# Row sums of layer 3's second four heads: matmul strips instead of accumulating DMAs, in a re-ordered four-layer graph network

## The chip, the core and the metric

The kernel runs on one NeuronCore of one Trainium2 chip. The core has engines with instruction queues of their own: TensorE (matmuls; PE in the profile, its weight loads PEld), VectorE (DVE), ScalarE (ACT), GpSimd (POOL) and SyncE (SP, which here only issues DMAs). GpSimd issues DMAs too: indirect gathers and scatters, and DMAs that add to what lies at the destination. The metric is the time of one launch in microseconds on the device.

## The reference, cut to what matters

The input is `x`, 32 samples of 512 nodes with 256 features, and an adjacency matrix of 512 x 512 that all samples share. Four layers follow one another, each as `x = x + layer(relu(layernorm(x)))`: layer 0 is masked attention with four heads of 64, layer 1 an MLP with two graph attention steps, layer 2 graph attention with four heads of 64, and layer 3 graph attention with eight heads of 32. Layer 3 is the one that changes:

```python
e = leaky_relu(e_src[..., :, None] + e_dst[..., None, :], 0.2)
e = e + (beta * log(adj + 1e-6))[:, None, :, :]
e = where(adj > 0, e, neg_inf)
attn = softmax(e, axis=-1)
h = einsum('bhij,bhjf->bhif', attn, x_proj)
x = x + (h in node order) @ W_out.T
```

The softmax has a numerator (weights times values) and a denominator, the row sum of the weights over all 512 keys. How the row sums are formed is what the change touches.

## The kernel before, in words

All work of one sample is written down as steps (`Step`), one per instruction or per small group of matmuls (`q.unit`), by `layer0` to `layer3` for each of the 32 samples. Nothing is issued then. `Plan.order` afterwards simulates the engines with the costs of `cost` and `transfer` and picks, again and again, the step that can start earliest, ties by its due time. `Plan.issue` writes the instructions in that order to all engines. So each engine's instruction order is fixed when the kernel is built, steps of up to seven samples lie between one another, and the semaphores hold an engine wherever the order was too hopeful. Due times come from `PERIOD` (the distance of samples), the longest chain behind the step, and `URGENT`, a table of corrections by tile name and layer; `STARTS`, `PACE` and `LAYERS` say from when a sample and a layer may run. A step starts only where buffers are free: 60 blocks of 128 x 512 fp32 in SBUF (tag `block`: p, total, R, raw and so on share them) and the eight PSUM banks (tag `bank`). A tile holds its buffer until its last reader is done.

For DMAs the planner keeps `landed`, the landing times of the last eight transfers of SP, and starts no SP transfer before the eighth-last has landed (`LANES = 8`). GpSimd's transfers are not held back in this way.

`separable` is the attention of layers 2 and 3. Heads go in groups of four: layer 2 has one group (g = 0), layer 3 two (g = 0 and 1). For each group, four row vectors are spread to all partitions by DMA (`R`), and for each of four key blocks j of 128 keys, and each of the group's four heads s, ScalarE forms `p[s]` (an exponential, 128 keys x 512 queries) and VectorE applies the maximum and the mask. TensorE then multiplies each `p[s]` with that head's values, as four strips of 32 columns side by side into one bank `av` (layer 2: two banks of strips of 64), accumulated over j. The row sums come in three ways:

- `direct`: four more strips behind those of the values, with a matrix of ones as weights, in each key block, into a bank `sm` accumulated over j. Before the change this is used for the last sample in layer 2 and the last two samples in layer 3 (`q.left`).
- `total`, group 0 otherwise: VectorE adds the four key blocks into four blocks; one set of four strips with ones then sums over partitions.
- group 1 of layer 3 otherwise: the key blocks j = 1 to 3 are added into the block of j = 0 (`first[s]`) by a DMA that GpSimd issues (`accum_op=ALU.add`), 12 per sample; one set of strips with ones follows.

`bars` hands the banks on: in layer 3 `normalise` copies them, sends the sums through DRAM for reciprocals, and multiplies. Layer 1 has the gathers that matter for the queues: rows are sorted by an indirect scatter (`order`), partial sums are written to a table in DRAM (`table`), and two gathers per 128 nodes (`g`, and `u`, which adds to what ScalarE wrote) fetch them; all of those are GpSimd's.

Of the kernel before, what the change touches and what calls it, by code (L numbers as in the profile page):

```python
# [18 lines left out]
ALU = mybir.AluOpType  # L19
# [15 lines left out]
H2, F2 = 4, 64  # L35
# [11 lines left out]
NO_TIES = float(N * (N * N - 1) // 3 - N) / 8.0  # L47


PERIOD = 190.0  # L50
STARTS, PACE = (0.0, 0.0, 111.0, 97.0), 58.0
LAYERS = (0.0, 42.0, 210.0, 99.0)

URGENT = {
    "stats:0": -40, "mv:0": -105, "ve:0": 445, "ms:0": -472, "h:0": 223, "pt:0": -138, "hT:0": -14, "qT:0": -396,
    "kT:0": 47, "v0:0": -81, "x:0": -388, "sc:0": 167, "p0:0": 112, "total:0": 519, "av:0": 239, "sm:0": 244,
    "sums:0": -217, "raw:0": 302, "s1:0": -35, "few:0": 258, "s2:0": 28, "oT:0": -33, "stats:1": -176, "mv:1": 83,
    "ve:1": 388, "rs:1": -39, "ms:1": -22, "h:1": -80, "pt:1": 220, "hT:1": 117, "mm:1": -251, "o1:1": -437,
    "nd1:1": -275, "w1:1": -438, "at:1": -24, "base:1": 129, "pick:1": -46, "sq1:1": -121, "ew:1": -778,
    "order:1": -382, "ds1:1": -77, "v1s:1": 27, "ab:1": 187, "past:1": 22, "sm:1": -279, "sums1:1": 471,  # L60
    "table:1": -176, "tab:1": -290, "wn:1": 118, "wt:1": 1, "tot:1": -436, "u1:1": -116, "g1:1": 274, "rs1:1": -121,
    "e:1": -164, "o2:1": -159, "o3:1": 109, "sd2:1": 213, "mx:1": 14, "nd:1": -162, "mn:1": -531, "ew2:1": -312,
    "p2:1": -367, "rs2:1": 79, "x:1": -10, "stats:2": -124, "mv:2": 29, "ve:2": -153, "rs:2": -5, "ms:2": 36,
    "h:2": 1050, "pt:2": 595, "hT:2": -1041, "mm:2": -208, "vs:2": -267, "es4:2": -266, "e4:2": 326, "rT:2": -98,
    "rd:2": -127, "R:2": 139, "p3:2": -454, "av:2": -38, "total:2": -340, "sm:2": 736, "y3:2": -2, "r4:2": 37,
    "ue:2": -16, "x:2": 1013, "stats:3": 8, "mv:3": 232, "ve:3": -469, "rs:3": 537, "ms:3": -6, "h:3": 469,
    "pt:3": -169, "hT:3": -9, "mm:3": -72, "vs:3": -142, "es8:3": 52, "e8:3": -385, "rT:3": 515, "rd:3": 238,
    "p3:3": -694, "av:3": -383, "total:3": 20, "sm:3": -205, "sums:3": -183, "raw:3": -72, "s1:3": -228, "few:3": 284,
    "s2:3": 34, "rc:3": -59, "oT:3": 35, "x:3": 136, "ai:3": -27, "af:3": 267, "top:3": 339, "values:3": 260,
    "rows:3": 598, "gp:3": 56, "gram:3": 954, "gab:3": -291, "sq:3": -187, "tp:3": 221, "res:3": -290,  # L70
}
BLOCKS, KEEP = 60, 2
KEEP_BANKS = 0
# [15 lines left out]
class Plan:  # L89
# [97 lines left out]
    def order(self):  # L187
# [27 lines left out]
        live, at = set(), {e: 0.0 for e in self.ENGINES.values()}  # L215
# [3 lines left out]
                if not step.waits:  # L219
                    open_[step.engine].append(step)  # L220
        result, count, mode = [], sum(map(len, self.samples)), "full"
        moved, landed = 0.0, [0.0] * self.LANES
        oldest = 0

        def slots(step):
# [24 lines left out]
        while len(result) < count:  # L250
            best = None
            for engine, waiting in open_.items():
                for step in waiting:
                    if step.sample > oldest + self.AHEAD:
                        continue
                    start = max(at[engine], step.ready)
                    if engine == "PE" and step.mode != mode:
                        start = max(start, at[engine] + self.SWITCH[mode])
                    if engine == "SP":
                        start = max(start, landed[0])  # L260
                    if best is not None and self.key(start, step) >= best[0]:
                        continue
                    when = slots(step)
                    if when is None:
                        continue
                    start = max(start, when)
                    if best is None or self.key(start, step) < best[0]:
                        best = self.key(start, step), start, step
            assert best is not None, "the buffers do not suffice"
            _, start, step = best  # L270
            step.start = start
            if lent and start >= FILLED_TO:
                free["block"] += [FILLED_TO] * lent
                lent = 0
            open_[step.engine].remove(step)
            at[step.engine] = start + step.busy
            if step.engine == "PE":
                mode = step.mode
            end = start + step.lasts
            if step.transfer:  # L280
                moved = max(moved, start + self.SETUP) + step.transfer
                end = max(end, moved + self.NOTICE)
            if step.engine == "SP":
                landed = landed[1:] + [end]
            for name in step.touches:
                tag, s = self.tile_tag[name], step.sample
                if name not in live:
                    live.add(name)
                    free[tag].pop(0)
                    held[s, tag] = held.get((s, tag), 0) + 1  # L290
                    to_come[s][tag] -= 1
                    pending[s, tag].remove(place[name])
                left[name] -= 1
                if not left[name]:
                    live.discard(name)
                    held[s, tag] -= 1
                    free[tag].append(end + self.HOP)
            for n in step.after:
                n.waits -= 1
                n.ready = max(n.ready, start + step.busy if n.engine == step.engine == "PE" else end + self.HOP)  # L300
                if not n.waits:
                    open_[n.engine].append(n)
            result.append(step)
            while oldest < len(self.samples) and not any(to_come[oldest].values()) and not any(
                n for (s, _), n in held.items() if s == oldest
            ):
                oldest += 1
# [123 lines left out]
def gnn_stack_kernel(ctx: ExitStack, tc: tile.TileContext, a: dict, out: bass.AP):  # L431
# [13 lines left out]
    x = a["x"]  # L445
# [49 lines left out]
    r2 = w2[:, :, 3 * H2 + D :]  # L495
# [183 lines left out]
    def pipelined(stack):  # L679
# [4 lines left out]
        q = Plan(nc, PERIOD)  # L684
# [454 lines left out]
        def separable(xt, w, nh, mask, bars):  # L1139
# [18 lines left out]
            for g in range(nh // 4):  # L1158
                R = blocks("R", 4)
                for s in range(4):  # L1160
                    q.sync.dma_start(R[s], rd[4 * g + s : 4 * g + s + 1, :].to_broadcast([P, N]))
                avs = [bank("av") for _ in range(4 // per)]
                direct = q.left <= (1 if nh == H2 else 2)
                total = blocks("total", 4) if g == 0 and not direct else None
                sm = bank("sm") if direct else None
                for j in range(NT):
                    p = blocks("p3", 4)
                    for s in range(4):
                        h = 4 * g + s
                        q.scalar.activation(p[s], R[s], AF.Exp, bias=e[:, j, h : h + 1])  # L1170
                        q.vector.scalar_tensor_tensor(
                            p[s], p[s], e[:, j, nh + h : nh + h + 1], mask[:, j, :], op0=ALU.max, op1=ALU.mult
                        )
                        if j and total:
                            q.vector.tensor_tensor(total[s], first[s] if j == 1 else total[s], p[s], op=ALU.add)
                        elif j and not direct:
                            q.gpsimd.dma_start(out=first[s], in_=p[s], accum_op=ALU.add)
                    if not j:
                        first = p
                    st = dict(start=(j == 0), stop=(j == NT - 1))  # L1180
                    with q.unit("columns", (0.86 if per == 4 else 1.72) + (0.86 if direct else 0)):
                        for s in range(4):
                            h, r0 = 4 * g + s, s % per * f
                            q.tensor.matmul(avs[s // per][r0 : r0 + f, :], half(v, j)[:, h * f : (h + 1) * f], p[s], **st)
                        if direct:
                            for s in range(4):
                                q.tensor.matmul(sm[s * F3 : (s + 1) * F3, :], ones[:, :F3], p[s], **st)
                if not direct:
                    sm = bank("sm")
                    with q.unit("columns", 0.86):  # L1190
                        for s, b in enumerate(total or first):
                            q.tensor.matmul(sm[s * F3 : (s + 1) * F3, :], ones[:, :F3], b, start=True, stop=True)
                bars(g, avs, sm)

# [560 lines left out]
```

## Time and profile before

| what | value |
|---|---|
| median of the three runs shown | 4038.0 us (4036.72 to 4048.28) |
| the profiled execution | 4047.94 us, span 4046.1 us |
| mean granted TensorE clock | 0.972 |
| busy: TensorE, VectorE, ScalarE, GpSimd | 3801.4, 3254.5, 3223.5, 1095.8 us |
| DMA queue of GpSimd | 212.13 MB, 26.8% of the 16 engines' span |
| DMA queue of SP | 284.88 MB, 22.5% |
| accumulating DMAs `p<-p` | 360 of 256 KB |

In the profile nearly every instruction has line 331, where `Plan.issue` makes it, so work is told apart by tile names: `p<-R,e` is ScalarE's exponential, `p<-p,e,mask3T` VectorE's mask step of layer 3, `av<-p,vs 128*32` a strip of values in layer 3 (`128*64` in layer 2), `sm<-p,ones` a strip of row sums taken from the weights (or from `first`), `sm<-total,ones` one taken from `total`. Every fp32 matmul shows as two records. In the waits, "X <- Y: a, n, b" means that X stood idle for a us in n waits, the longest b, until Y was done. The last 260 us or so are a drain: the last samples have no others to run beside.

### The profile page before, as it was taken

The page shows a single profiled execution, that of the slowest core. Times are in us where ns is not written, and L with a number is a line of the kernel's source. Part 1 is how long each engine was busy: PE and PEld are TensorE (multiplying, and loading weights), DVE is VectorE, ACT ScalarE, POOL GpSimd, SP SyncE. Part 2 cuts the span into 40 slices and gives each one's busy share as a digit, 9 for nine tenths or more (in the row PEclk, how much of TensorE's full clock was granted, in tenths as well). Part 3 has the DMA queues.
Part 4 walks back from the last instruction along what each step waited for, and adds up shares of the span by engine and source line. Part 5 has one row for each costly group of instructions (what it writes and reads, how often), then busy time and mean ns, then how long its engine had stood idle before and what let it go on. Part 6 is the DMA issues. An engine that isn't in the chain of part 4 may idle for free. (4 is left out here: it accounts for less than half of the span.)

```text
span 4046.1 us, 59455 instructions
## 1 busy us (share of the span) xinstructions
PE 3801.4 (94%) x17691; PEld 2185.6 (54%) x17691; DVE 3254.5 (80%) x8161; ACT 3223.5 (80%) x7120; POOL 1095.8 (27%) x1016
## 2 busy tenths in 40 slices
PE   8999999999999999999999999999999999989787
PEld 4655564655646465564655646465464654636443
DVE  5477888879788797887879878797887879869687
ACT  3679788788888878788788887878788788868775
POOL 1213223141222413213232222513223132141310
PEclk9999999999999999999999999999999999989898
DMA  3426446463544736445464553736446464453631
GB/s 96 135 48 168 100 130 148 109 177 82 150 114 111 179 85 168 102 139 129 110 161 95 147 120 96 192 79 164 93 127 157 103 170 97 124 130 90 184 85 60
DMA packets 365761, 501.16 MB, mean 124 GB/s; under 512 B 114043, under 2 KB 167550, under 8 KB 365430
## 3 DMA queue, kind: packets, MB, share of 16 engines
q0 software_dynamic: 107776, 212.13, 26.8%
q1 hardware_dynamic: 257380, 284.88, 22.5%
q8 instruction: 144, 2.36, 0.2%
q14 instruction: 187, 1.53, 0.1%
q10 hardware_dynamic: 274, 0.26, 0.0%
HBM read 263.84 MB, written 122.13 MB: 95 GB/s over the span
## 5 line engine op out<-in xcount | busy, mean ns | idle before, releaser
L331 ACT ACTIVATE p<-R,e 128x512 f32<-128x512 f32 x1536 | 1000.9, 729 | 23.1 <-DMA R<-rd 17.4
L331 DVE SCALAR_TENSOR_TENSOR p<-p,e,mask3T 128x512 f32<-128x512 f32 x1024 | 719.5, 743 | 56.3 <-ACT p L331 33.9
L331 POOL DMA_DIRECT2D p<-p x360 | 341.0, 1258 | 1015.5 <-ACT v L331 732.6
L331 PE MATMUL av<-p,vs 128*32 128x512 f32 (+1 forms) x3072 | 540.8, 602 | 28.5 <-DVE p L331 27.6
L331 POOL TENSOR_TENSOR rs<-ve,mhalf 128x4 f32<-128x4 f32 x128 | 176.7, 1380 | 1199.4 <-DVE ve L331 961.5
L331 PE MATMUL mm<-W_fc,o 128*128 128x256 f32 (+1 forms) x2048 | 497.2, 380 | 0.0
L331 DVE TENSOR_TENSOR total<-total,p 128x512 f32<-128x512 f32 x744 | 490.1, 684 | 0.0
L331 PEld LDWEIGHTS mm<-W_fc,o 128*128 128x128 f32 x2048 | 370.0, 190 | 75.1 <-issue 23.9
L331 DVE TENSOR_TENSOR p<-p,mask0T 128x512 f32<-128x512 f32 x512 | 330.0, 685 | 88.6 <-ACT p L331 87.1
L331 DVE SCALAR_TENSOR_TENSOR p<-p,e,mask1T 128x512 f32<-128x512 f32 x512 | 364.1, 739 | 42.6 <-ACT p L331 40.6
L331 ACT ACTIVATE h<-x,ms,rs 128x256 f32<-128x256 f32 x512 | 269.7, 598 | 83.0 <-DVE ms L331 81.5
L331 PEld LDWEIGHTS av<-p,vs 128*32 128x32 f32 (+1 forms) x3072 | 135.2, 118 | 359.4 <-issue 220.4
L331 ACT ACTIVATE p<-sc 128x512 f32<-128x512 f32 x512 | 269.6, 649 | 40.4 <-DMA p<-p 22.3
L331 PE MATMUL mm<-w,hT 128*128 128x272 f32 (+1 forms) x1024 | 271.8, 407 | 18.1 <-ACT p L331 12.7
L331 POOL DMA_INDIRECT g<-table,pick x128 | 205.8, 1608 | 227.2 <-ACT v L331 79.2
L331 POOL DMA_INDIRECT u<-table,pick x128 | 229.0, 1789 | 134.5 <-ACT u L331 75.8
L331 PE MATMUL sc<-qT,kT 64*128 64x512 f32 x1024 | 262.2, 636 | 0.0
L331 PE MATMUL av<-p,v 128*64 128x512 f32 x1024 | 252.6, 610 | 4.2 <-ACT u L331 2.6
L331 DVE TENSOR_TENSOR total<-p,p 128x512 f32<-128x512 f32 x372 | 246.3, 684 | 9.4 <-DMA p<-p 7.1
L331 PE MATMUL mm<-hT,mlp_w 128*128 128x512 f32 x512 | 244.5, 600 | 0.5 <-ACT hT L331 0.5
L331 PE MATMUL av<-v,p 128*128 128x257 f32 x1024 | 237.9, 385 | 4.1 <-DVE p L331 3.7
L331 PE MATMUL mm<-o,mlp_w 128*128 128x512 f32 x512 | 240.6, 616 | 0.9 <-DVE x L331 0.4
(236 smaller groups left out, 7126.1 us busy)
## 6 DMA issues: line engine op xcount, KB each, us to landing
R<-rd SPq DMA_DIRECT2D x384, 256.0 KB
p<-p POOLq DMA_DIRECT2D x360, 256.0 KB
table<-tab SPq DMA_DIRECT2D x256, 256.0 KB
v1s<-order SPq DMA_DIRECT2D x128, 256.0 KB
x<-in_x_dram SPq DMA_DIRECT2D x32, 512.0 KB
x<-boa POOLq DMA_DIRECT2D x32, 512.0 KB
rc<-s SPq DMA_DIRECT2D x128, 128.0 KB
out_dram<-x SPq DMA_DIRECT2D x32, 512.0 KB
```

The source lines that it names most:

```text
L331: inst = getattr(getattr(self.nc, attribute), op)(*args, **kw)
```

## The change

The second group of layer 3 takes the direct form for all samples. The accumulating DMA goes, and with it the case that the final set of strips reads `first`. The planner counts GpSimd's transfers as it counts SP's: eight in flight, kept apart by engine. The constants of the order are others. `cost` and `transfer` are as before. The diff, with the table of urgencies cut:

```diff
-PERIOD = 190.0
-STARTS, PACE = (0.0, 0.0, 111.0, 97.0), 58.0
-LAYERS = (0.0, 42.0, 210.0, 99.0)
+PERIOD = 107.0
+STARTS, PACE = (0.0, 0.0, 40.0, 20.0), 71.0
+LAYERS = (0.0, 68.0, 39.0, 132.0)

 URGENT = {
-    "stats:0": -40, "mv:0": -105, "ve:0": 445, "ms:0": -472, "h:0": 223, "pt:0": -138, "hT:0": -14, "qT:0": -396,
+    "stats:0": 115, "mv:0": -234, "ve:0": 358, "rs:0": 194, "ms:0": 199, "h:0": -83, "pt:0": -186, "hT:0": 211,
...
-        moved, landed = 0.0, [0.0] * self.LANES
+        moved, landed = 0.0, {e: [0.0] * self.LANES for e in ("SP", "POOL")}
...
-                    if engine == "SP":
-                        start = max(start, landed[0])
+                    if step.transfer:
+                        start = max(start, landed[engine][0])
...
             if step.transfer:
                 moved = max(moved, start + self.SETUP) + step.transfer
                 end = max(end, moved + self.NOTICE)
-            if step.engine == "SP":
-                landed = landed[1:] + [end]
+                landed[step.engine] = landed[step.engine][1:] + [end]
...
-                direct = q.left <= (1 if nh == H2 else 2)
+                direct = g == 1 or q.left <= (1 if nh == H2 else 2)
...
-                        elif j and not direct:
-                            q.gpsimd.dma_start(out=first[s], in_=p[s], accum_op=ALU.add)
...
-                        for s, b in enumerate(total or first):
+                        for s, b in enumerate(total):
                             q.tensor.matmul(sm[s * F3 : (s + 1) * F3, :], ones[:, :F3], b, start=True, stop=True)
```

## The prediction

> **What bounds the kernel now.** I read the page first, then busy time by stretch, then the waits of TensorE and ScalarE in the steady part, and last the timeline around one stall. The page says which engine is full:
>
> ```profile
> span 4046.1 us, 59455 instructions
> PE 3801.4 (94%) x17691; PEld 2185.6 (54%) x17691; DVE 3254.5 (80%) x8161; ACT 3223.5 (80%) x7120; POOL 1095.8 (27%) x1016
> ...
> L331 POOL DMA_DIRECT2D p<-p x360 | 341.0, 1258 | 1015.5 <-ACT v L331 732.6
> ```
>
> TensorE is busy for 94% of the span, VectorE and ScalarE for 80%, GpSimd for 27%. So a step on TensorE costs its own length unless it falls into a hole, and GpSimd time is worth nothing by itself. The written order repeats every two samples, 245 us, in the middle of the kernel (columns: stretch, length, then busy us with counts for PE, PEld, DVE, ACT, POOL, then granted clock, DMA share, GB/s):
>
> ```profile
> 1757.00:2002.00 245.00, 233.25 (x1083) 134.51 (x1082) 201.93 (x503) 199.01 (x434) 71.12 (x63) 0.97 0.51 127
> 2002.00:2247.00 245.00, 232.97 (x1090) 133.59 (x1089) 201.60 (x501) 199.85 (x443) 71.16 (x65) 0.98 0.52 128
> ```
>
> TensorE stands still for some 12 us of each (10.8 on the mean of six such stretches). Who ends that idle time, from 400 to 3700 us:
>
> ```profile
> PE mm L331 <- DVE u L331: 36.4, 13, 2.8
> PE pt L331 <- DVE u L331: 32.0, 28, 4.2
> PE mm L331 <- ACT hT L331: 20.0, 12, 1.8
> PE mm L331 <- ACT p L331: 12.7, 15, 1.6
> PE mm L331 <- ACT tab L331: 7.5, 9, 1.8
> ```
>
> and, one step further back, what held ScalarE up in the same stretch:
>
> ```profile
> ACT tab L331 <- DMA table<-tab: 24.0, 12, 2.9
> ACT tab L331 <- DMA p<-p: 23.1, 13, 7.3
> ACT p L331 <- DMA p<-p: 22.3, 19, 2.1
> ```
>
> The accumulating transfer hurts here: it holds its source and destination blocks until it lands, and ScalarE waits for a block to write. One instance in the timeline:
>
> ```profile
> 2086.47 0.60 ACT L331 ACTIVATE p<-sc 128x512 f32<-128x512 f32 x1 [1.86 <-DMA p<-p]
> 2087.12 1.18 PE L331 MATMUL mm<-w,hT 128*128 128x272 f32 x4 [1.31 <-ACT p L331]
> 2088.73 1.18 PE L331 MATMUL mm<-w,hT 128*128 128x272 f32 x4 [0.43 <-ACT p L331]
> ```
>
> ScalarE is 1.86 us late, and TensorE loses 1.31 and 0.43 us behind it, once per two samples.
>
> **The change, part by part.** *Matmul strips added.* Samples 0 to 29 (30 of them) take the direct form in the second group of layer 3; the last two have it already. Their price stands at the end of the trace, where those two run it:
>
> ```profile
> 4020.48 1.06 PE L331 MATMUL av<-p,vs 128*32 128x512 f32 x8
> 4021.36 1.04 PE L331 MATMUL sm<-p,ones 128*32 128x512 f32 x8
> 4022.22 1.35 PE L331 MATMUL av<-p,vs 128*32 128x512 f32 x7
> ```
>
> Starts are 0.88 and 0.86 us apart: a set of four row-sum strips (8 records) right behind its value strips holds TensorE for 0.86 us. Four key blocks make 3.44 us per sample. *Matmul removed:* the single row-sum set at the end of the group. Such a set starts at 2092.79 and the next matmul at 2093.78, so 0.99 us goes. Net 2.45 us per sample, times 30: **+73.5 us**. The holes ahead of value strips cannot take it: in 400 to 3700 us, av waits for DVE p only 10.6 us in 14 waits, the longest 0.8.
>
> *Accumulating DMAs removed*, 12 per sample, 360 in all. Their 341.0 us of GpSimd hide behind its 73% of idle time, so they give nothing directly. They move 360 x 256 KB = 94 MB of the 212 MB of GpSimd's queue, which holds 26.8% of the DMA engines' time; by bytes that is some 12% of it. What TensorE gets back is the stall above: mm waits of 12.7 and 7.5 make **-20 us**. The ends are 0 (ScalarE is next held by its own table<-tab waits of 24.0) and -51 (all of ScalarE's p<-p waits: 23.1, 22.3 and 5.4 for vs). I take what reached TensorE.
>
> *Drain.* From 3818.8 to 3833.05 us TensorE idles 4.93 + 8.80 us, and the chain of waits there is GpSimd issuing four accumulations (3.69 us), 1.95 us of issue and 8.06 us of one landing; that is 13.7 us. **-14 us**; the ends are 0 (the layer-1 gathers beside it are as late) and -14.
>
> *GpSimd's queue counted.* The planner now starts no GpSimd transfer before the eighth-last has landed, so gathers and the steps behind them are placed later in all four engines' orders. VectorE waits 71.3 us for the gather u in 400 to 3700, and TensorE's 32.0 us of pt behind DVE u follow. After such a hole TensorE is slow: the four sc matmuls at 2140.94 took 2.08 us, those at 2102.31 took 1.14, so 0.94 per two samples, 13 us over 14 pairs. That is 45 us in all. The gathers' own times stay as the planner's cost lines have them, and in one group (issued at 2105.73 and 2108.12, used at 2112.80 and 2116.67) they came 7.1 and 8.6 us after issue with no accumulation issued for 15 us before, so I take half: **-22 us**, ends 0 and -45. The Trainium skill, "TensorE: Matmul & The Clock Gate", in its part on the HAM clock gate, says that the clock falls back only after some 3.4 us without work; the hole here was 1.88 us, so the measurement differs; by that rule the 13 us would be no part of it, and the sum would come out 6 us higher.
>
> *A PSUM bank held longer.* The row sums' bank is now taken from the first key block on: in one sample the strips ran from 2062.79 to the sum at 2092.79, 30 us of some 122. The nearest row for lack of a bank is mm behind DVE u (36.4 us: the output projection waits for VectorE to empty one). A quarter of that, **+9 us**; ends 0 and +36, since the planner may place around it.
>
> *New constants.* Period, starts, layer offsets and the table of urgencies move nearly every step on all five queues, SP's and GpSimd's too. No step is added. The trace cannot price it; it is bounded by the idle time. To close all of it would give -146 us (10.8 x 13.5 pairs), to double it +146. I take nothing beyond the terms above, and keep part of these ends in the range. VectorE and ScalarE keep every instruction, and their cover is 20% idle time each.
>
> Sum against the profiled execution: 4047.94 + 73.5 - 20 - 14 - 22 + 9 = 4074. That execution stood 9.9 us above the median of the runs shown (4038.0), so I forecast **4064 us**, 0.65% slower.
>
> **Rivals.** *Faster, by run-ahead.* The blocks are what decides: 60 of them; each accumulation holds a source for the 8.06 us seen above, or 10.84 us for another in the chain, four destinations are held through the group, and ScalarE stood 51 us waiting for one. With them free the planner can keep more ready work in front of TensorE. What can be won is 146 us of idle and what slow matmuls follow it: per two samples 0.94 at 2140, 1.36 at 2185 (the projection took 2.82, against 1.46 elsewhere) and 1.9 after 2106, 4.2 x 13.5 = 57, together 203 us. It decides from the point where more than 73.5 - 14 + 12 = 72 us, about a third, comes back. At half: 4038 + 73.5 - 14 - 101 = 3997 us. For it: ScalarE's waits. Against it: the larger holes name VectorE and ScalarE work of layers 0 and 1 (2.79 us behind DVE u, 1.76 behind ACT hT), which no accumulation delays in the timeline. Beside it, the Trainium skill, "DMA: Bandwidth & Descriptors", in "Issuing engines are not separate DMA queues", says that all issuers share the same 16 engines, so that SP's loads would land sooner too; no run here shows that yet.
>
> *Nothing comes back.* The stalls move to the next late thing, the table writes or the gathers, and the bank costs its 9: 4038 + 73.5 + 9 - 5 = 4115 us, with 5 of the drain's 14. For it: ACT tab waits as long for table<-tab (24.0) as for p<-p (23.1).
>
> *Even.* The strips are as real as forecast, but the gathers give all 45 and ScalarE's stalls 40: 4038 + 73.5 - 40 - 45 - 14 + 9 = 4022 is just past even; with less of it, 4026 to 4050. That the strips are not added, or cost nothing, I leave out: the holes for them are not there.
>
> **Numbers.** Chances: forecast 0.42 (own range 4050 to 4090), faster by run-ahead 0.39, nothing back 0.11, even 0.08. A measurement of this kernel tells about 0.3% (12 us) from no change; the three runs shown span 0.29%. So slower 0.53, same 0.08, faster 0.39. The range holds 8 in 10: it reaches down to 3985, past the half-way case, and up to 4100, short of the last rival.
>
> **What would show it.** Right: sm<-p,ones grows from 400 to 400 + 30 x 24 = 1120 records, p<-p is gone from GpSimd, busy PE in a two-sample stretch rises by about 5 us, waits of ACT on DMA p<-p vanish, and waits of PE on DVE u shrink but stay. Wrong: TensorE busy above 96.5% in the middle with a span below 4026 means that run-ahead won; DVE u waiting on gathers as long as before means that term is nil; new waits of mm on whoever empties banks, above 20 us more, mean that the bank is worth more than 9.

## The result, and the profile after

The changed kernel takes **3988.75 us** (median of four, 3985.92 to 3993.38) against 4037.36 us before: a ratio of 0.9881, 95% interval 0.9852 to 0.9910. It is 48.6 us faster; I had forecast it 26 us slower, at 4064. The time lies inside the range given, at its low end, on the side of the rival.

The page of the kernel after, its span, its busy times with their counts, and the queue of GpSimd's DMAs (packets, MB, share of the 16 engines' span):

```profile
span 3983.8 us, 59611 instructions
...
PE 3802.1 (95%) x18411; PEld 2192.6 (55%) x18411; DVE 3262.9 (82%) x8161; ACT 3209.5 (81%) x7120; POOL 814.3 (20%) x658
...
q0 software_dynamic: 55936, 117.73, 13.7%
```

TensorE has 720 matmul records more, as forecast, and yet its busy time is 0.7 us more, not 73.5. Its idle time (span less busy) fell from 4046.1 - 3801.4 = 244.7 to 181.7 us. So the whole gain is idle time, 63 us, and something ate the length of the strips inside "busy". Groups of TensorE by form show where: busy us, mean ns of one, then the idle time ahead of them. `mm<-woT,oT` is layer 0's output projection, `mm<-w,hT 128x272` layer 3's projection, `pt<-ident,h` the transposes of the normalised rows, `av<-p,v` layer 0's weighted values. The line of `Plan.issue` lies between 330 and 338, depending on the kernel. First before, then after:

```profile
L331 PE MATMUL av<-p,vs 128*32 128x512 f32 x2048 | 307.4, 601 | 16.0 <-DVE p L331 15.2 <-DVE u L331 0.4 <-DVE rs L331 0.3
...
L331 PE MATMUL pt<-ident,h 128*128 128x128 f32 x1024 | 175.6, 283 | 20.7 <-ACT h L331 19.7
L331 PE MATMUL mm<-woT,oT 128*128 128x256 f32 x512 | 141.8, 419 | 40.3 <-DVE u L331 36.4 <-DVE oT L331 3.9
L331 PE MATMUL mm<-w,hT 128*128 128x272 f32 x512 | 141.8, 425 | 17.3 <-ACT p L331 12.7 <-ACT tab L331 2.2 <-ACT vs L331 1.5
```

```profile
L330 PE MATMUL av<-p,vs 128*32 128x512 f32 x2048 | 279.5, 597 | 2.7 <-DVE p L330 2.1 <-DVE rs L330 0.5
L330 PE MATMUL av<-p,v 128*64 128x512 f32 x1024 | 278.0, 630 | 47.4 <-DVE rs L330 31.4 <-DVE p L330 16.0
...
L330 PE MATMUL sm<-p,ones 128*32 128x512 f32 x1120 | 158.4, 594 | 0.0
L330 PE MATMUL pt<-ident,h 128*128 128x128 f32 x1024 | 156.9, 280 | 19.1 <-ACT h L330 15.3 <-ACT sums L330 3.3 <-ACT u L330 0.2
...
L330 PE MATMUL mm<-w,hT 128*128 128x272 f32 x512 | 130.3, 405 | 3.4 <-ACT hT L330 3.4
...
L330 PE MATMUL mm<-woT,oT 128*128 128x256 f32 x512 | 121.3, 380 | 0.9 <-DVE oT L330 0.9
```

The same matmuls, in the same number, were busy 27.9, 18.7, 20.5 and 11.5 us less in four of these groups (`av<-p,vs`, `pt<-ident,h`, `mm<-woT,oT`, `mm<-w,hT`). Of the unchanged matmuls, the group that went furthest the other way is `av<-p,v` (252.6 before, idle 4.2). In the two `mm` groups, which stood behind holes, the single matmul is shorter than it was (419 and 425 ns before, 380 and 405 after), so busy time holds a part of the holes' price. In `av<-p,vs` the mean hardly moves (601 and 597), so there the matmuls lie closer together. A group's busy time also depends on what the order puts between its matmuls, so a single group's difference is not a price.

The waits of TensorE from 400 to 3700 us, after (waited for: us, times, longest):

```profile
PE pt L330 <- DVE u L330: 33.0, 21, 2.6
PE av L330 <- DVE rs L330: 32.0, 12, 4.4
PE mm L330 <- DVE oT L330: 8.4, 14, 1.3
PE sm L330 <- DVE past L330: 7.7, 10, 1.3
PE av L330 <- DVE p L330: 6.4, 4, 2.7
```

The 36.4 us of `mm` behind DVE u are gone and the 20.0 behind ACT hT nearly so; 32.0 us of `av` behind DVE rs are new; the 32.0 of `pt` behind DVE u stayed. In windows of 400 us from 400 to 3600 TensorE was busy for 95.4% before and is for 96.9% after (sums of eight windows over 3200 us); one of the eight, before and after:

```profile
2000.00:2400.00 400.00, 380.84 (x1762) 211.19 (x1761) 318.25 (x809) 330.80 (x738) 126.40 (x113) 0.98 0.55 137
```

```profile
2000.00:2400.00 400.00, 386.35 (x1853) 215.91 (x1850) 337.28 (x822) 340.08 (x744) 88.58 (x69) 0.98 0.41 111
```

### The profile page after: what moved, and what is told of

It reads as the page before. It is cut to its first block, busy times and chain, and to the rows that moved or that the text cites. A ratio compares the mean times of both kernels' runs of the same rounds, so it can differ in the third digit from the quotient of the medians.

```text
span 3983.8 us, 59611 instructions
## 1 busy us (share of the span) xinstructions
PE 3802.1 (95%) x18411; PEld 2192.6 (55%) x18411; DVE 3262.9 (82%) x8161; ACT 3209.5 (81%) x7120; POOL 814.3 (20%) x658
## 4 chain that ended last, share of the span: by engine, by line
PE 57%; ACT 13%; DVE 13%; DMA 9%; issue 4%; POOL 1%; SPq 1%; DVEq 0%; POOLq 0%; ACTq 0%
PE mm L330 30%; PE av L330 15%; PE pt L330 6%; ACT p L330 5%; PE sm L330 4%; DMA u<-table,pick 4%; DVE p L330 4%; DVE total L330 3%; PE sc L330 2%; ACT e L330 2%; DVE u L330 2%; DMA rc<-s 2%; DMA R<-rd 1%; SPq L330 1%; ACT w L330 1%
## 5 line engine op out<-in xcount | busy, mean ns | idle before, releaser
L330 ACT ACTIVATE p<-R,e 128x512 f32<-128x512 f32 x1536 | 1036.3, 739 | 23.9 <-DMA R<-rd 15.7
L330 POOL TENSOR_TENSOR rs<-ve,mhalf 128x4 f32<-128x4 f32 x128 | 192.3, 1502 | 1729.1 <-DVE ve L330 1711.0
L330 PE MATMUL av<-p,vs 128*32 128x512 f32 (+1 forms) x3072 | 519.8, 601 | 11.3 <-DVE p L330 6.4
L330 PE MATMUL mm<-W_fc,o 128*128 128x256 f32 (+1 forms) x2048 | 483.8, 380 | 0.0
L330 ACT ACTIVATE h<-x,ms,rs 128x256 f32<-128x256 f32 x512 | 278.5, 607 | 67.3 <-DVE ms L330 66.2
L330 PE MATMUL av<-p,v 128*64 128x512 f32 x1024 | 278.0, 630 | 47.4 <-DVE rs L330 31.4
L330 POOL DMA_INDIRECT order<-v,at x128 | 157.9, 1233 | 505.8 <-ACT v L330 392.6
L330 PE MATMUL mm<-w,hT 128*128 128x272 f32 (+1 forms) x1024 | 253.3, 399 | 4.1 <-ACT hT L330 4.1
L330 PE MATMUL sc<-qT,kT 64*128 64x512 f32 x1024 | 251.6, 627 | 0.1
L330 POOL DMA_INDIRECT g<-table,pick x128 | 175.5, 1371 | 285.5 <-DMA rc<-s 104.1
```

The costliest lines, as they stand in the source:

```text
L330: inst = getattr(getattr(self.nc, attribute), op)(*args, **kw)
```

## The experiments

Three things change at once: the transfers go, the strips come, and the order is another. **Theory** after the result: the transfers cost far more than the waits that name them, since the matmuls behind such a wait are slow too. **Rival one:** the new order did it, and the transfers are worth about the 34 us (stalls and drain) that I gave them. **Rival two:** the strips cost less than their length. The first runs separate the three by doing one part at a time. Where kernels of different launches are compared, I use their ratios to the kernel before of the same launch, times 4040 us.

**The transfers alone.** The order before, with the 360 accumulating DMAs not issued; the row sums of the second group then hold key block 1 only. `before_no_accumulation`:

```diff
                 for attribute, op, args, kw in step.calls:
+                    if "accum_op" in kw and self.kinds.get(kw["out"].tensor.name) == "p3":
+                        continue
```

> The kernel before, its order kept step for step, without the 360 accumulating transfers: the row sums of the second group then hold the first key block alone. Theory 'transfers' (holding the blocks costs far more than the 20 us that the waits named): 3980 us or less, 57 us or more under the kernel before. Theory 'order' (the gain lies in where the steps stand, and the transfers cost what the forecast took, 20 to 34 us with the drain): 4003 to 4017 us. Theory 'strips are cheap' says nothing on this run.

Measured: 3958.44 us, ratio 0.9790 (0.9771 to 0.9809), so the transfers cost **85 us** in an order that was made with them. Both kernels issue the same matmuls in the same sequence, so start can be compared with start. (The spans of the two profiled executions lie 97 us apart, and the figures from traces belong to these.) The distance between them grows steadily up to the drain, from 6.2 us at 800 us to 31.1 at 2000, 65.5 at 3200, 87.0 at 3600 and 99.7 at 4000. One place where it grows is the one that the prediction showed. Its matmuls in the timeline of TensorE, before, and without the transfers (start, length, count, idle time ahead):

```profile
2083.06 2.74 PE L331 MATMUL av<-v1s,w 64*128 64x512 f32 x12
2087.12 1.18 PE L331 MATMUL mm<-w,hT 128*128 128x272 f32 x4 [1.31 <-ACT p L331]
2088.73 1.18 PE L331 MATMUL mm<-w,hT 128*128 128x272 f32 x4 [0.43 <-ACT p L331]
2090.26 2.49 PE L331 MATMUL mm<-w,hT 128*128 128x272 f32 x8 [0.35 <-ACT tab L331]
2092.59 0.27 PE L331 MATMUL pt<-ident,wn 128*128 128x128 f32 x1
```

```profile
2051.20 2.74 PE L333 MATMUL av<-v1s,w 64*128 64x512 f32 x12
2053.87 3.93 PE L333 MATMUL mm<-w,hT 128*128 128x272 f32 x16
2057.64 0.27 PE L333 MATMUL pt<-ident,wn 128*128 128x128 f32 x1
```

From the first of these lines to the last it is 9.53 us with the transfers and 6.44 without: 3.09 us for two samples. The named idle time is only 1.31 + 0.43 + 0.35 = 2.09. Nearly all of the other 1.00 us is that the pieces of 4, 4 and 8 matmuls took 1.18 + 1.18 + 2.49 = 4.85 us, where 16 in one stream took 3.93. The forecast had read 1.31 + 0.43 here. ScalarE, in the timeline before, is stopped four times at this one place, not once:

```profile
2086.47 0.60 ACT L331 ACTIVATE p<-sc 128x512 f32<-128x512 f32 x1 [1.86 <-DMA p<-p]
...
2088.08 0.60 ACT L331 ACTIVATE p<-sc 128x512 f32<-128x512 f32 x1 [0.92 <-DMA p<-p]
2089.62 0.58 ACT L331 COPY tab<-av 128x512 f32<-128x512 f32 x1 [0.95 <-DMA p<-p]
...
2091.14 0.65 ACT L331 COPY vs<-mm 128x256 f32<-128x256 f32 x2 [0.66 <-DMA p<-p]
```

Over the whole trace the group `mm<-w,hT` got 16 us less busy and 17 us less idle by it. The second place is `av<-p,vs`, whose wait is for VectorE, which a reading of TensorE's waits by name does not put down to a transfer:

```profile
L333 PE MATMUL av<-p,vs 128*32 128x512 f32 x2048 | 288.8, 601 | 8.1 <-DVE p L333 7.6 <-DVE u L333 0.4
...
L333 PE MATMUL mm<-w,hT 128*128 128x272 f32 x512 | 126.0, 399 | 0.5 <-ACT hT L333 0.5
```

The two places make 33 and 26 us of the 97, from start to start; the rest is spread (14 us at `pt<-ident,h`, 11 at `sm<-p,ones`, whose weight loads before the change wait 8.8 us for the transfer itself, 10 at `av<-v1s,w`, and less). How the stall passes from ScalarE through VectorE to `av<-p,vs` was not followed step by step.

Rival one's 34 us are refuted. VectorE's wait for the gather u fell from 71.3 to 54.2 us in this run, but TensorE's wait behind it stayed (32.0 to 31.1 for `pt`, 36.4 to 36.3 for `mm`), so TensorE gained nothing from that.

**Bytes or number.** The same 360 DMAs, cut to a quarter of their columns; they hold the same blocks, and GpSimd issues as many. `before_quarter_columns`:

```diff
-                            q.gpsimd.dma_start(out=first[s], in_=p[s], accum_op=ALU.add)
+                            q.gpsimd.dma_start(out=first[s][:, :P], in_=p[s][:, :P], accum_op=ALU.add)
...
```

The lines that are not shown keep the planner's costs as they were, so that the order stays.

> The order before, kept, with each of the 360 accumulating transfers cut to a quarter of its columns, 64 KB instead of 256 (row sums are then right for a quarter of the queries). Count, places and held blocks are the same. Theory 'time of the transfer' (bytes through the DMA engines, until which the blocks are held): most of the 85 us goes, 3965 to 3995 us. Theory 'a fixed price for each transfer' (issue, queue, the wait for its end): 4020 us or above.

```profile
L331 POOL DMA_DIRECT2D p<-p x360 | 344.6, 1506 | 950.5 <-ACT v L331 718.6
...
p<-p POOLq DMA_DIRECT2D x360, 64.0 KB
```

```profile
ACT tab L331 <- DMA table<-tab: 7.8, 12, 1.8
```

```profile
L331 PE MATMUL av<-p,vs 128*32 128x512 f32 x2048 | 300.8, 603 | 14.7 <-DVE p L331 14.6
...
L331 PE MATMUL mm<-w,hT 128*128 128x272 f32 x512 | 126.4, 400 | 0.5 <-ACT hT L331 0.5
```

Measured: 3980.05 us, ratio 0.9856 (0.9823 to 0.9888). GpSimd's issue time is what it was (344.6 us), and 58 of the 85 us are back. So the larger part of the price goes with the bytes. The other 27 us are not the price of the number alone, since a quarter of the bytes is still moved: if the price were one part for the number and one in proportion to the bytes, 85 and 27 would make these parts some 8 and 77 us, an estimate that no further run supports. The stall at `mm<-w,hT` is fully gone, the one at `av<-p,vs` mostly not.

The bytes can cost in two ways: the blocks are held until the transfer lands, and other transfers land later beside it. The traces show both. ScalarE's waits on `p<-p` are the first. For the second, ScalarE's wait for the table writes (`tab` behind DMA table<-tab, from 400 to 3700 us) is 24.0 us before, 7.8 here, and is no longer among its waits without the transfers. By the semaphore records of the three traces, the median table write between 400 and 3700 us landed 6.5, 4.1 and 3.1 us after its issue, while the row vectors (`R<-rd`) took about 5 us in all three. No run holds the blocks without moving the bytes, so how the 85 us are shared between the two stays open.

**The strips alone.** The order before, no transfers, and strips for key blocks 2 to 4 issued right behind those of the values, added into the values' bank, so that no bank is held longer (the second group's values then hold these sums too). `before_strips_in_place`:

```diff
...
+                        if g == 1 and j and not direct:
+                            for s in range(4):
+                                q.tensor.matmul(avs[0][s * F3 : (s + 1) * F3, :], ones[:, :F3], p[s], start=False, stop=(j == NT - 1))
```

> The order before, kept step for step, without the accumulating transfers, and with the new strips of key blocks 1 to 3 in samples 0 to 29 put behind the value strips of the same key block: 30 x 3 x 0.86 = 77.4 us of TensorE. They are added into the bank of the values, so that no further bank is held (the values of the second four heads then have row sums added, and their row sums hold one key block). The comparison is with the same order without transfers and strips, which took 3958 us. Theory 'the strips cost their length': 4035 us, and the new order is then worth some 45 us of the gain. Theory 'the strips find slack in any order' (as they did in the order after, where leaving three of four out saved 6 us): 3990 us or less, and the new order is worth nothing but that the bank fits.

```profile
span 4028.7 us, 59833 instructions
...
PE 3830.9 (95%) x18411; PEld 2194.5 (54%) x18411; DVE 3252.0 (81%) x8161; ACT 3228.6 (80%) x7120; POOL 742.7 (18%) x656
```

Measured: 4027.5 us, ratio 0.9956 (0.9938 to 0.9974). Against the run without transfers that is 0.0166 of 4040, **67 us** for 90 sets of 0.86 = 77.4. In this order the strips cost 87% of their length, and rival two falls here. Strips into a bank of their own were not tried in the order before, which keeps no bank for them from the first key block on. With the constants of before the planner finds no order for the changed steps, since no buffer comes free, and with the new constants it finds none for the steps of before; so the constants and the held bank have no separate price.

**The strips in the new order.** The kernel after, with three of four sets of strips not issued (again key block 1 only), `after_one_key_block`; and with each set issued twice, `after_strips_twice`:

```diff
+                    strip = (
+                        op == "matmul" and step.layer == 3 and step.sample < 30
+                        and self.kinds.get(args[0].tensor.name) == "sm" and not (kw["start"] and kw["stop"])
+                    )
+                    if strip and not kw["start"]:
+                        continue
...
```

> The kernel after, its order kept, with the new row-sum strips of the first key block alone in samples 0 to 29 (the row sums leave out key blocks 1 to 3): 30 x 3 sets of 0.86 us are gone, 77.4 us. If the strips cost their length, 3911 us (3900 to 3922). Theory 'strips are cheap' (they lie in holes of TensorE): 20 to 40 us less than the kernel after, 3949 to 3969 us.

> The kernel after, its order kept, with each new set of row-sum strips issued twice (the row sums of these heads come out doubled): 30 x 4 x 0.86 = 103.2 us of TensorE more. If the strips cost their length, 4092 us (4080 to 4104). Theory 'strips are cheap': half of that or less, 4040 us or below.

Measured: 3982.55 us, ratio 0.9849 (0.9830 to 0.9868), and 4054.61 us, ratio 1.0029 (1.0011 to 1.0047). Taking 77.4 us of strips away gives 6 us by the medians, 13 by the ratios; the intervals of the two overlap. That is less than either theory had allowed (3949 to 3969 us was the higher range). Adding 120 sets, 103.2 us, costs 60 by the ratios, 66 by the medians, which lies between the theories. So in the new order the strips that are there stand for the most part in time that TensorE would lose anyway; more of them do cost. Where it goes when they are taken away, TensorE's groups in that run:

```profile
L338 PE MATMUL sc<-qT,kT 64*128 64x512 f32 x1024 | 269.0, 645 | 0.2
...
L338 PE MATMUL pt<-ident,h 128*128 128x128 f32 x1024 | 163.5, 282 | 25.1 <-ACT h L338 21.0 <-ACT sums L338 3.3 <-ACT u L338 0.4
...
L338 PE MATMUL av<-v1s,w 64*128 64x512 f32 x512 | 131.2, 609 | 3.0 <-DVE ue L338 1.5 <-ACT rT L338 0.2
```

With the strips these groups were busy for 251.6, 156.9 and 121.7 us. The scores (`sc`) and the sums `av<-v1s,w` of layer 1 wait for others inside their busy time: hardly any idle time is named ahead of them (0.2 and 3.0 us). Whether they wait for ScalarE to empty a bank I only infer.

**The transfers in the new order.** The kernel after with the 360 DMAs beside the strips (their result is not read), `after_with_accumulation`; and in place of the strips of key blocks 2 to 4, `after_accumulation_for_strips`:

```diff
+                    if g == 1 and j and q.left > 2:
+                        for s in range(4):
+                            q.samples[-1][-1].calls.append(
+                                ("gpsimd", "dma_start", (), dict(out=first[s], in_=p[s], accum_op=ALU.add))
+                            )
```

> The kernel after, its order kept, with the 360 accumulating transfers put back as dead weight behind each key block's matmuls (they add into blocks that nothing reads any more, so the output stays). Theory 'transfers': 57 us or more over the kernel after, 4046 us or above. Theory 'order': 20 to 34 us over it, 4009 to 4023 us.

> The order after, kept, with the second group's work of the kernel before in it: accumulating transfers instead of the strips of key blocks 1 to 3 (the row sums hold the first key block alone). Theory 'the transfers cost, the strips don't': as with both, within 30 us of 4235, that is 4205 to 4240 us. Theory 'the 246 us came from transfers and strips together, TensorE being full': 77 us less, 4158 us or below.

Measured: 4235.37 us, ratio 1.0471 (1.0438 to 1.0505), and 4254.74, ratio 1.0533 (1.0499 to 1.0567): 238 and 263 us more than the kernel after (the second is 15 us above the range that was expected). The page's DMA issue line of the first (size, median us from issue to landing), and two waits in it from 400 to 3700 us:

```profile
p<-p POOLq DMA_DIRECT2D x360, 256.0 KB, 6.0
```

```profile
PE av L330 <- DVE p L330: 52.4, 38, 3.1
```

```profile
DVE u L330 <- DMA u<-table,pick: 166.5, 39, 8.4
```

After, the same two waits are 6.4 and 85.7. The same DMAs cost 85 us where the order was made with them, and three times that where it was not: here the planner knows neither their time on GpSimd nor how long they hold their blocks. So this order is good only without the transfers. It does not say what an order with the new constants, planned with the transfers, would give.

**GpSimd's queue counted.** The kernel after, with the planner counting SP's transfers only, as before. `after_uncounted`:

```diff
-        moved, landed = 0.0, {e: [0.0] * self.LANES for e in ("SP", "POOL")}
+        moved, landed = 0.0, [0.0] * self.LANES
...
```

> The kernel after with the planner counting SP's transfers alone, as before. All theories: the planner gives the same order of all 25,236 steps with and without the count, so 3980 to 3995 us, as the kernel after.

Measured: 3978.64 us, one time. The planner gives the same order of all steps with the count and without it, both here and with the steps and constants of before. (The 25,236 steps of the expectation are those of before; after the change there are 360 transfers and 30 final sets fewer, 24,846.) So this part of the change does nothing, and the 10 us between 3978.64 and 3988.75 are spread between launches.

**The order.** Three kernels that differ from the kernel after in the order alone, or nearly: 18 urgencies changed, two of them new, all but `vs:2` (by 412) by less than 150; the distance of samples 120 in place of 107; and the direct form in layer 2 for the last two samples.

```diff
-    ... "tot:1": -7, ... "mm:2": -112, "vs:2": -78, ... "vs:3": -642, ... "rows:3": -325, ...
+    ... "tot:1": -81, ... "mm:2": -134, "vs:2": 334, ... "vs:3": -583, ... "rows:3": -471, ...
```

```diff
-PERIOD = 107.0
+PERIOD = 120.0
```

```diff
-                direct = g == 1 or q.left <= (1 if nh == H2 else 2)
+                direct = g == 1 or q.left <= 2
```

> The kernel after with 18 entries of the table of urgencies changed by small amounts, so that the same 25,236 steps go out in another order: 8% of TensorE's steps stand more than ten places from where they stood. Nothing is added or left out. The kernel's own planner ends this order 30.6 us later than the one it has (3763.7 against 3733.0 by its costs). What is asked is where the 39 us between strips in the order before (4027.5) and the kernel after (3988.75) lie. Theory A (the order was fitted to these steps, and the planner's figure carries over): the time is 3988.75 + 30, 4010 to 4030, with as many half-clock stretches as before, about 200 us. Theory B (any order that this planner makes for steps without accumulating transfers is about as good, since nothing lands late any more): 3980 to 4000, half-clock stretches about 165 us. Theory C (orders this close together differ by chance on the chip, the planner ranks them no finer than some 20 us): anywhere from 3965 to 4010, without a relation to the planner's figure.

> The kernel after with one constant changed, the distance of samples 120 in place of 107, and the table of urgencies as it is. The same steps, nothing left out; the planner ends this order 216 us later than its own (3949.3 against 3733.0). Theory A (the constants fit each other and the steps; one moved alone loses what the search found): 3988.75 + 216 x 0.9 to 1.1, 4180 to 4230. Theory B (without accumulating transfers any order is about as good): 3980 to 4060. The forecast's term for new constants was 0 with ends of 146 to both sides; this run measures one end of it.

> The kernel after with the direct form in layer 2 for the last two samples in place of the last one. For one sample more, 16 additions of VectorE give way to strips of TensorE (some 4 x 1.3 us more). The planner ends it 2.7 us later. If TensorE's own work sets the time: +4 us, about 3993. If VectorE's work in the drain sets it: 16 x 0.6 us less on VectorE, at best -8, about 3981. If the order alone decides: anything from 3970 to 4010.

Measured: 4001.29 us, ratio 0.9895 (0.9852 to 0.9938); 4250.09 us, one time; 3984.63 us, ratio 0.9848 (0.9806 to 0.9891). One constant of the planner moved by 12% costs 261 us by the times, 248 against the kernel before of its own launch, with the same steps; theory A had 4180 to 4230. The page of that run:

```profile
span 4248.4 us, 59620 instructions
...
PE 3917.6 (92%) x18411; PEld 2236.3 (53%) x18411; DVE 3268.2 (77%) x8161; ACT 3233.9 (76%) x7120; POOL 795.8 (19%) x657
```

Theory B, that any order without transfers is about as good, falls with it. The nearby order came out 12.5 us later (6 by the ratios), below theory A's range and within theory C's: the planner's 30.6 us did not carry over, but these intervals do not say more. The last kernel can't be told from the kernel after, so none of these beats it. The half-clock time, which I had taken for a sign of a good order, is no measure either: summed over the trace's records of the granted clock it is 224.7 us before, 164.5 after, and 138.1 in the nearby order, which is not faster; in `after_uncounted`, the same order as after, it is 144.0.

## Why the prediction was wrong

| term | forecast | shown by |
|---|---|---|
| strips | +73.5 | +67 in the order before |
| ScalarE's stalls and drain | -20 - 14 | -85 in the order before, drain included |
| GpSimd's queue counted | -22 | no effect on any step |
| bank held longer | +9 | not separated from the order |
| new constants | 0 | -30 (0.9881 less 0.9956, of 4040), bank included |
| sum | +26 | -48 |

By the intervals of the ratios, the three measured terms are good to some 8, 11 and 14 us (transfers, strips, constants). They are the steps of one path, from the order before; in the order after the same parts have other prices.

- **What bounds the kernel.** "A step on TensorE costs its own length unless it falls into a hole" held in the order before (87%), not in the new one, where 77.4 us of strips are worth 6 to 13. A busy share of 95% does not show that TensorE is the bound. The Trainium skill, "Perfetto Trace Analysis", in "Identifying the Most-Contended Engine", says that matmul busy share is not a good measure of how close a kernel is to its roofline. The traces agree as far as they go: it was 95% with these strips and without them.
- **Matmul strips added.** Count (400 to 1120 records) and length (0.86 us a set) were right.
- **Accumulating DMAs removed** is the step that failed, by its size. I took "what reached TensorE": the `mm` waits that lead back to the transfer by name. That left out the slow matmuls behind each hole (16 of the 33 us at `mm<-w,hT`) and what reached TensorE through VectorE (`av<-p,vs`, 26 us less start-to-start time in the run without transfers). In place of the -34 for stalls and drain the runs showed -85. All of ScalarE's waits on the transfer, the end that I gave as -51, would have been nearer, and was itself no bound. The end of 0 rested on the table writes holding ScalarE next (24.0 us); these waits went away with the transfers.
- **Drain.** -14 is borne out: from 3600 to 4000 us, which holds the drain, the distance between the two traces grows by 12.7 us.
- **GpSimd's queue counted.** The mechanism was wrong. Nothing is placed elsewhere by the count, VectorE's wait for u rose from 71.3 to 85.7 us, and TensorE's behind it (`pt`, 33.0) stayed, as the prediction's own sign for a term of nothing had it.
- **New constants.** "I take nothing", with ends of 146. The kernel gained some 30 with the bank, and with one constant moved it loses some 250, so idle time was no bound: in that run TensorE is busy for 3917.6 us, 115.5 more than after, with the same matmuls, and idle for 330.8 in place of 181.7. That the constants had to be others, with the bank held through the group, the prediction did not see.
- **Rivals.** *Faster, by run-ahead* named the right cause, the transfers, and its half-way time of 3997 is 8 us from the result; its sign (over 96.5% busy in the middle, a span under 4026) is what was seen, at 96.9%. Its mechanism is not what was shown: without any new order, the transfers' removal alone gives 85 us, and that run shows the sign too (96.6%, span 3949.5). That its time came so near is partly luck: its 14 and 101 us for the drain and closed holes stand where the runs put 85 on the transfers and 30 on the order. That SP's transfers would land sooner, which it left open, is shown for the table writes. My argument against it, that the larger holes belong to layers 0 and 1, was true (36.4 and 36.3 us behind DVE u with and without the transfers) and beside the point, as the time lay in the smaller holes and behind them; it is the new order that closed these 36 us. *Nothing comes back* and *Even* are refuted.
- **What would show it.** ScalarE's waits on `p<-p` are gone, as forecast. "Busy PE rises by 5 us in two samples" was wrong, since busy time fell elsewhere by as much. New waits of `mm` on whoever empties banks, above 20 us, did not come (8.4 us behind DVE oT is the longest entry of `mm` after).

## What to carry to other kernels

The price of a transfer that holds buffers is not the sum of the waits that name it: count the whole stretch, from the last matmul that was on time to the next one that is back in its stream, and follow the late engine to the others that it feeds. Where an order is fixed when the kernel is built, a step's price belongs to the order (the strips 67 or 6 to 13 us, the transfers 85, or about 250 in an order planned without them), and a change that comes with a new order should have a range that is as wide as orders differ, not as wide as the idle time. To learn what a part is worth, take it out of the old order first and leave the order alone.

## What was not expected of the hardware

The 360 accumulating DMAs between SBUF blocks, 26.8 - 13.6 = 13.2% of the DMA engines' time with and without them, cost the kernel 85 us although their issue hid on GpSimd; at a quarter of the bytes and the same count they cost 27 us. SP's table writes landed in about half the time without them (a median of 3.1 us in place of 6.5).

TensorE's clock often falls to half behind short holes. Windows of TensorE before (length, busy and count, granted clock, DMA share, GB/s), around the hole of 1.88 us that ends at 2140.30:

```profile
2138.00:2141.00 3.00, 1.12 (x10) 0.96 0.84 107
2141.00:2144.00 3.00, 3.00 (x7) 0.50 0.43 73
2144.00:2147.00 3.00, 3.00 (x8) 0.97 0.00 0
```

In that trace all five holes of 1.8 to 2.2 us and 15 of 16 of 2.2 to 3 us have a half-clock record that starts no later than 10 us behind them; of the 17 of 1.5 to 1.8 us four, of the 19 of 1.2 to 1.5 us nine. After the change it is six of eight and nine of 17 in the first two ranges, so a hole's length alone does not decide it. The Trainium skill, "TensorE: Matmul & The Clock Gate", in its part on the HAM clock gate, has half rate after at least one idle window of about 3.4 us; these holes are shorter, so the measurement differs. Without the transfers the half-clock time fell only from 224.7 to 210.8 us, so the clock is a small part of what they cost.
